# A router whose weights are stationary, with four token tiles in four column groups, and a gate summed on VectorE

## The chip, the cores and the metric

The kernel runs on one core of a Trainium2 chip. The metric is device time in microseconds: the median of the runs. The profile is of one execution. Engines in it: PE is TensorE's matmuls, PEld its weight loads, DVE is VectorE, ACT is ScalarE, POOL is GpSimd, SP is SyncE, whose queue issues most DMAs.

## The reference

4096 tokens (16 sequences of 256) of 256 channels pass a feed-forward layer, an attention layer and the same feed-forward layer again. Cut to what matters here:

```
x = x + 0.5 * ffn(layernorm(x))
x = x + attention(layernorm(x))       # 16 heads, 8 for keys and values, of 32; causal, tanh cap
x = x + 0.5 * ffn(layernorm(x))

def ffn(inp):
    h = w_norm * inp * rsqrt(mean(inp * inp) + 1e-6)
    probs = softmax(h @ w_router)                     # 256 x 32: 32 experts
    weight, chosen = top_k(probs, 4)
    out = sum over the chosen experts e, first 128 tokens of each:
          weight * (silu(h @ w_gate[e]) * (h @ w_up[e])) @ w_down[e]      # width 176
    sh = (silu(h @ sw_gate) * (h @ sw_up)) @ sw_down                      # shared expert, width 704
    return inp + out + sigmoid(h @ w_shared_gate) * sh                    # w_shared_gate: 256 x 1
```

All numbers are fp32. The change concerns `h @ w_router` and `h @ w_shared_gate`.

## The kernel before

The activations `x` stay in SBUF as 32 tiles of 128 tokens. Eight groups (`g`) of four tiles (`GT`) are the unit of routing. `route(n, g)` does one group of feed-forward layer `n` in pieces (it is a generator; a caller that advances it decides what lies between the pieces):

- moments of the four tiles on VectorE (L220, L221), their roots on GpSimd (L227, L228);
- `xr`, the rows without their mean and scaled, on VectorE (L248);
- eight transposes on TensorE into `pt` (L257), which ScalarE copies to `xnT`, times `w_norm` (L260); ScalarE also brings `x` to its normalised form (L268);
- the logits `pl` (L276): for each tile and each half of the channels one matmul, with the tile's 128x128 block of `xnT` as the stationary side and 33 columns of `wr` moving: 32 of the router and one of the shared gate;
- VectorE copies `pl` to `lg` (L280), takes the gate's column out of it (L281), then the maximum `mx` (L283) and `ex = lg - mx` (L285); ScalarE takes the exponential (L287);
- VectorE makes probabilities `pr` (L290 to L297), GpSimd puts them behind `xr` and a DMA writes both to the table `xtab` in HBM, from which experts gather rows; VectorE finds the top four and the `mask` (L303 to L307).

`slots` turns masks into lists of rows (its first matmul is `pc`, from `mask`); `expert` does one expert. `shared(g)` is the shared expert for a group: six steps of four matmuls `pg` (L390) with their activation `act` (tanh on ScalarE L394; L395 and L396 on VectorE), then four steps `po` (L402) whose sum goes to `x` (L406), scaled by `sg`, a tanh of the gate (L376). These steps serve as filling work on TensorE: `Fill.take(us)` issues steps until so many microseconds are used, and `ROUTE_FILL` and its like say how many between two pieces of another stage.

Order: TensorE follows the program's order throughout. In the first feed-forward layer a scheduler orders VectorE and ScalarE; in the attention stage all of TensorE, VectorE, ScalarE and GpSimd follow the program's order. The routing of layer 0 is the span's first 116 us, groups one after another with filling work between. The routing of layer 1 is done inside the attention loop, one piece at a time between scores (`sc`, L552), values (`den` and `y`, L598), projections (`project`: `pv` L531 with copies `v` L535, `pq` L503) and the output projection (`poa`, L616, L620). Five of its groups stand directly ahead of `pv`; groups 5 and 6 come at about 744 and 778 us, group 7 after the loop at 798 us.

PSUM: the pool `ps1` gives two buffers to everything with the tag `mm`: `pt`, `pl`, `po`, `pv`, `pq`, `poa`, `pta`, `pte`, `pc`. Whoever takes the third waits until the first is read.

## Time and profile before

| | us |
|---|---|
| median of 3 runs | 1070.91 (1069.13 to 1072.49) |
| the profiled execution | 1070.05 |
| its span | 1068.3, at a mean granted TensorE clock of 0.995 |
| TensorE busy | 1031.8 |
| VectorE busy | 628.8 |
| GpSimd busy | 499.3 |
| ScalarE busy | 399.9 |

TensorE's busy time by stage: first routing, 55.90 of the first 62 us and 53.47 of the 54 up to 116 us; experts of layer 0, 342.85 of 354 us (116 to 470); attention, 249.20 of 250 us (470 to 720) and 71.97 of 80 (720 to 800), the routing's tail among them; experts of layer 1, 228.74 of 234 us (800 to 1034); the last 34.3 us, 29.68.

A row of a group of instructions reads: line, engine, operation, output<-inputs with partitions x elements and type, how many | busy us of all, mean ns of one | idle time before them, and what ended it. The chain lists start, duration and work in the order of time; the timeline start, duration, engine, line and operation. An fp32 matmul has two records.

### The profile page before, as it was taken

What the parts mean: (1) busy time and instruction counts of PE and PEld (TensorE: products, weight loads), DVE (VectorE), ACT (ScalarE), POOL (GpSimd) and SP (SyncE); (2) the same over time, 40 slices, a digit from 0 to 9 for tenths busy, and PEclk for the clock granted to TensorE, in tenths of its full rate; (3) what the DMA queues carried; (4) which work ended last, traced back from release to release, by engine and by line L of the source; (5) the groups of instructions that cost most, each with busy time, mean ns of one, the idle gap of its engine ahead of it and who ended that gap; (6) DMA issues with size and microseconds to landing.
All of it is one profiled execution on the core that took longest, in us unless ns stands there. A gap on an engine that the chain in (4) does not pass through costs nothing.

```text
span 1068.3 us, 15597 instructions
## 1 busy us (share of the span) xinstructions
PE 1031.8 (97%) x5432; PEld 650.7 (61%) x5432; DVE 628.8 (59%) x1681; ACT 399.9 (37%) x761; POOL 499.3 (47%) x552
## 2 busy tenths in 40 slices
PE   9999999999999899999999999998999999999998
PEld 5657656777767544545455556554466567767675
DVE  5755664445343457777778777774556744443434
ACT  3343111222221246675658475756621112221210
POOL 4500102555542298788476767562311024545536
PEclk9999999999999999999999999999999999999999
DMA  9811701778773000000101010000030027777739
GB/s 297 243 69 45 233 12 48 170 159 172 168 164 58 30 21 1 20 21 2 42 1 42 2 43 1 23 1 23 25 82 23 6 56 157 163 153 170 167 55 314
DMA packets 137869, 92.97 MB, mean 87 GB/s; under 512 B 80512, under 2 KB 135104, under 8 KB 137792
## 3 DMA queue, kind: packets, MB, share of 16 engines
q1 hardware_dynamic: 125504, 74.16, 24.9%
q0 software_dynamic: 12288, 17.83, 9.7%
q8 instruction: 43, 0.70, 0.3%
q14 instruction: 34, 0.28, 0.1%
HBM read 60.99 MB, written 30.97 MB: 86 GB/s over the span
## 4 chain that ended last, share of the span: by engine, by line
PE 89%; DVE 6%; ACT 3%; issue 1%; DMA 0%; SPq 0%; POOL 0%; ACTq 0%; POOLq 0%
PE pg L390 28%; PE po L402 14%; PE pge L437 8%; PE pq L503 8%; PE poa L616 5%; PE poe L450 5%; PE sc L552 5%; PE y L598 3%; PE den L598 3%; PE pv L531 3%; PE pl L276 2%; PE pte L429 1%; PE pt L257 1%; DVE act L395 1%; DVE act L396 1%
## 5 line engine op out<-in xcount | busy, mean ns | idle before, releaser
L390 PE MATMUL pg<-xnT,sw 128*128 128x512 f32 x704 | 320.7, 600 | 1.8 <-ACT p L559 1.8
L390 PEld LDWEIGHTS pg<-xnT,sw 128*128 128x128 f32 x704 | 131.1, 192 | 138.8 <-issue 130.7
L453 POOL DMA_INDIRECT acc<-y,idx x64 | 101.4, 1584 | 183.6 <-DVE y L452 104.8
L402 PE MATMUL po<-swd,act 128*128 128x256 f32 x768 | 179.9, 383 | 6.6 <-DVE act L396 2.4
L402 PEld LDWEIGHTS po<-swd,act 128*128 128x128 f32 x768 | 143.0, 190 | 35.7 <-issue 13.0
L395 DVE SCALAR_TENSOR_TENSOR act<-act,pg 128x512 f32<-128x512 f32 x96 | 65.7, 684 | 167.9 <-ACT act L394 167.8
L394 ACT ACTIVATE act<-pg 128x512 f32<-128x512 f32 x96 | 57.2, 596 | 271.3 <-PE pg L390 271.3
L559 ACT ACTIVATE p<-sc 128x512 f32<-128x512 f32 (+1 forms) x128 | 97.4, 808 | 106.8 <-PE sc L552 106.3
L564 POOL TENSOR_SCALAR_AFFINE_SELECT p<-p 128x512 f32<-128x512 f32 x128 | 82.3, 667 | 48.1 <-ACT p L562 45.7
L413 POOL DMA_INDIRECT xg<-xtab,idx x64 | 67.9, 1061 | 76.8 <-DVE idx L368 57.9
L437 PE MATMUL pge<-xgT,wgu 128*112 128x128 f32 (+1 forms) x768 | 95.8, 275 | 5.9 <-issue 4.4
L562 ACT ACTIVATE p<-p 128x512 f32<-128x512 f32 (+1 forms) x128 | 100.9, 844 | 0.0
L437 PEld LDWEIGHTS pge<-xgT,wgu 128*112 128x112 f32 (+1 forms) x768 | 88.8, 182 | 8.7 <-issue 7.6
L552 PE MATMUL sc<-qT,kT 32*128 32x256 f32 (+1 forms) x512 | 68.5, 535 | 4.7 <-DVE act L396 3.4
L406 DVE SCALAR_TENSOR_TENSOR x<-po,sg,x 128x256 f32<-128x256 f32 x64 | 30.8, 483 | 69.2 <-PE po L402 68.9
L396 DVE TENSOR_TENSOR act<-act,pg 128x512 f32<-128x512 f32 x96 | 65.7, 685 | 2.4
L511 POOL TENSOR_TENSOR qs<-qs,kc 128x512 f32<-128x512 f32 x48 | 61.2, 1275 | 12.7 <-DVE qs L506 12.7
L432 ACT ACTIVATE xgT<-pte,wnorm 128x128 f32<-128x128 f32 x128 | 39.8, 364 | 71.3 <-PE pte L429 71.3
L450 PE MATMUL poe<-wd,sie 112*128 112x256 f32 x256 | 66.0, 380 | 0.1
L616 PE MATMUL poa<-wo,yT 128*128 128x256 f32 x256 | 59.8, 386 | 2.1 <-DVE qT L510 1.2
L503 PE MATMUL pq<-hT,wq 128*128 128x512 f32 x128 | 60.9, 600 | 0.0
L616 PEld LDWEIGHTS poa<-wo,yT 128*128 128x128 f32 x256 | 47.3, 190 | 19.8 <-ACT xnT L260 5.0
(110 smaller groups left out, 1343.7 us busy)
## 6 DMA issues: line engine op xcount, KB each, us to landing
xtab<-xr SPq DMA_DIRECT2D x16, 576.0 KB
acc<-zero SPq DMA_DIRECT2D x2, 4224.0 KB
a<-acc SPq DMA_DIRECT2D x16, 512.0 KB
wgu<-in_L_ffn_w_gate SPq DMA_DIRECT2D x64, 112.0 KB
wgu<-in_L_ffn_w_up SPq DMA_DIRECT2D x64, 112.0 KB
wd<-in_L_ffn_w_down SPq DMA_DIRECT2D x64, 112.0 KB
wgu<-in_L_ffn_w_gate SPq DMA_DIRECT2D x64, 64.0 KB
wgu<-in_L_ffn_w_up SPq DMA_DIRECT2D x64, 64.0 KB
```

What stands on the lines that cost most here:

```text
L390: nc.tensor.matmul(pg[:, s, :], lhsT=sw[:, c, w0 : w0 + P], rhs=xnT[:, c, cols], start=(c == 0), stop=(c == 1))
L395: nc.vector.scalar_tensor_tensor(si, si, 1.0, pg[:fw, 0, :], ALU.add, ALU.mult)
L402: nc.tensor.matmul(po, lhsT=act[:, k, t * P : (t + 1) * P], rhs=swd[:, k, :], start=(k == 0), stop=(k == len(FC) - 1),)
L437: nc.tensor.matmul(pg[:fw, n_, :], lhsT=wgu[:, c, w0 : w0 + fw], rhs=xgT[:, c, :], start=(c == 0), stop=(c == 1))
L450: nc.tensor.matmul(po, lhsT=si[:, k, :], rhs=wd[:, k, :], start=(k == 0), stop=(k == 1))
L453: nc.gpsimd.indirect_dma_start(out=acc[n], out_offset=bass.IndirectOffsetOnAxis(ap=idx[:, e : e + 1], axis=0), in_=y, in_offset=None, boun ...
L503: nc.tensor.matmul(pq, lhsT=weights[:, c, :], rhs=hT[:, c, :], start=(c == 0), stop=(c == 1))
L552: nc.tensor.matmul(sc[i // 2][:, i % 2, 0 : 2 * w].rearrange("p (s t) -> p s t", s=2), lhsT=kT[r, m, t0 + k0 : t0 + k0 + P], rhs=qT[r, m, ...
L559: nc.scalar.activation(parts[h], sc[h][:, :, 0 : 2 * w], AF.Tanh, scale=QK_SCALE / SOFTCAP)
L562: nc.scalar.activation(parts[h], parts[h], AF.Exp, scale=SOFTCAP)
L564: nc.gpsimd.affine_select(out=diag, in_=diag, compare_op=ALU.is_ge, fill=0.0, base=0, pattern=[[0, 4], [1, P]], channel_multiplier=-1,)
L616: nc.tensor.matmul(po, lhsT=yT[:, c // 2, c % 2, qh * P : (qh + 1) * P], rhs=wo[:, c // 2, c % 2, :], start=(c == 0), stop=(c == 3),)
```

## The change

The logits are computed the other way round: the router's weights (128x32 for each half of the channels) are stationary, and a tile's 128 tokens move. The four tiles of a group go to four column groups of the array, partitions 32t to 32t+31 of `plt`. ScalarE copies `plt` to `lt`, one transpose on TensorE makes `pl` with tokens on the partitions, and VectorE reads `mx` and `ex` from PSUM. The gate's logit is a sum over channels on VectorE: `xr` times `wg` (the gate's weights times `w_norm`, on every partition), with the accumulator written to `gate`. `wg` takes two DMAs and a multiply; `w_norm` is parked in the last tile of `x`. There is one more `yield` in `route`, and filling work is dealt out anew around it. Constants: `triu` is made from a comparison, and `last` is one column.

```diff
-ROUTE_FILL, SLOT_FILL, ... = 3.0, 1.7, ...
+ROUTE_FILL, SLOT_FILL, ... = 2.0, 1.7, ...
+LOGIT_FILL = 2.5
...
-    wr = cpool.tile([P, 2, E + 1], F32, name="wr")
-    nc.sync.dma_start(wr[:, :, 0:E], w_router.rearrange("(c p) e -> p c e", p=P))
-    nc.sync.dma_start(wr[:, :, E : E + 1], w_shared_gate.rearrange("(c p) e -> p c e", p=P))
+    wr = cpool.tile([P, 1, 2, E], F32, name="wr")
+    nc.sync.dma_start(wr[:, 0], w_router.rearrange("(c p) e -> p c e", p=P))
...
+    wg = cpool.tile([P, C], F32, name="wg")
+    nc.sync.dma_start(wg, w_shared_gate.rearrange("c e -> e c").to_broadcast([P, C]))
+    nc.sync.dma_start(x[:, NT - 1, :], w_norm.unsqueeze(0).to_broadcast([P, C]))
+    nc.vector.tensor_mul(wg, wg, x[:, NT - 1, :])
     load_x(1)
...
-    nc.vector.tensor_copy(triu, const("triu"))
+    nc.vector.tensor_single_scalar(triu, const("iota"), slot, ALU.is_ge)
...
-        pl = ps1.tile([P, GT, E + 1], F32, tag="mm", name="pl")
+        plt = ps1.tile([P, 1, P], F32, tag="mm", name="plt")
+        for s in range(1):
+            for c in range(2):
+                for t in range(GT):
+                    i = g * GT + t
+                    nc.tensor.matmul(
+                        plt[E * t : E * (t + 1), s, :], lhsT=wr[:, s, c, :], rhs=xnT[:, c, i * P : (i + 1) * P],
+                        start=(c == 0), stop=(c == 1),
+                    )
+        lt = stat.tile([P, 1, P], F32, name="lt", bufs=1)
+        nc.scalar.copy(lt, plt)
         for t in range(GT):
             i = g * GT + t
-            for c in range(2):
-                nc.tensor.matmul(
-                    pl[:, t, :], lhsT=xnT[:, c, i * P : (i + 1) * P], rhs=wr[:, c, :], start=(c == 0), stop=(c == 1)
-                )
-        lg = stat.tile([P, GT, E + 1], F32, name="lg", bufs=2)
-        nc.vector.tensor_copy(lg, pl)
-        nc.vector.tensor_copy(gate[:, g * GT : (g + 1) * GT], lg[:, :, E])
+            junk = stat.tile([P, C], BF16, name="junk", bufs=1)
+            nc.vector.scalar_tensor_tensor(
+                junk, xr[:, t, 0:C], 1.0, wg, ALU.mult, ALU.mult, accum_out=gate[:, i : i + 1]
+            )
+        yield 0.8
+        pl = ps1.tile([P, 1, GT, E], F32, tag="mm", name="pl")
+        for s in range(1):
+            nc.tensor.transpose(pl[:, s].rearrange("p t e -> p (t e)"), lt[:, s, :], ident)
         mx = stat.tile([P, GT, 1], F32, name="mx")
-        nc.vector.tensor_reduce(mx[:, :, 0], lg[:, :, 0:E], AX.X, ALU.max)
+        nc.vector.tensor_reduce(mx[:, :, 0], pl[:, 0], AX.X, ALU.max)
         ex = stat.tile([P, GT, E], F32, name="ex", bufs=2)
-        nc.vector.tensor_sub(ex, lg[:, :, 0:E], mx.to_broadcast([P, GT, E]))
-        yield 1.9
+        nc.vector.tensor_sub(ex, pl[:, 0], mx.to_broadcast([P, GT, E]))
+        yield 0.2
...
-        nc.tensor.matmul(pn, lhsT=const("last"), rhs=hib.rearrange("p h i -> p (h i)"), start=True, stop=True)
+        nc.tensor.matmul(
+            pn, lhsT=const("last").to_broadcast([P, P]), rhs=hib.rearrange("p h i -> p (h i)"), start=True, stop=True
+        )
...
     def shared(pool, g, last):
-        sg = stat.tile([P, GT], F32, name="sg")
-        nc.scalar.activation(sg, gate[:, g * GT : (g + 1) * GT], AF.Tanh, scale=0.5)
-        nc.vector.tensor_scalar(sg, sg, 1.0, 0.125, ALU.add, ALU.mult)
...
         for k, (f0, fw) in enumerate(FC):
+            if k == 3:
+                sg = stat.tile([P, GT], F32, name="sg")
+                nc.scalar.activation(sg, gate[:, g * GT : (g + 1) * GT], AF.Tanh, scale=0.5)
+                nc.vector.tensor_scalar(sg, sg, 1.0, 0.125, ALU.add, ALU.mult)
...
             fill.take(ROUTE_FILL)
+            next(work)
+            fill.ready = g + 1
+            fill.take(LOGIT_FILL)
             advance(work, 2)
             advance(later[2])
-            fill.ready = g + 1
             fill.take(ROUTE_FILL)
             next(work)
...
+            if j == 1:
+                advance(routing.get(g - 2))
+                if mine is None:
+                    spare_time(LOGIT_FILL)
```

More of the change, by code (lines that the diff above doesn't have):

```diff
@@ L40 @@
 ET = mybir.EngineType
-ROUTE_FILL, SLOT_FILL, FIRST_FILL, EXPERT_FILL, SUM_FILL, PROJECT_FILL = 3.0, 1.7, 6.0, 2.4, 17.0, 1.5
+ROUTE_FILL, SLOT_FILL, FIRST_FILL, EXPERT_FILL, SUM_FILL, PROJECT_FILL = 2.0, 1.7, 6.0, 2.4, 17.0, 1.5
 LAST_FILL = 8.0
@@ L54 @@
 _n = 0
-for _name, _w in [("ident", P), ("cos", T), ("sin", T), ("triu", P), ("iota", CAP),
-                  ("ustrict", P), ("last", P), ("block", P // NT), ("slot", 1), ("spare", 1), ("base", 1)]:
+for _name, _w in [("ident", P), ("cos", T), ("sin", T), ("iota", CAP),
+                  ("ustrict", P), ("last", 1), ("block", P // NT), ("slot", 1), ("spare", 1), ("base", 1)]:
     _COLS[_name] = (_n, _w)
@@ L76, in _constants @@
     put("sin", np.tile(np.sin(emb).T * sign[:, None], (P // HD, 1)))
-    put("triu", np.triu(np.ones((P, P))))
     put("iota", np.tile(np.arange(CAP) + 0.5, (P, 1)))
@@ L83, in _constants @@
     put("ustrict", blocks * np.triu(np.ones((P, P)), 1))
-    put("last", np.tile(p % NT == NT - 1, (1, P)))
+    put("last", p % NT == NT - 1)
     put("block", p // NT == np.arange(P // NT))
```

## The prediction

> **What bounds the kernel now.** I read first the busy times and the chain that ended last, on the page.
>
> ```profile
> PE 1031.8 (97%) x5432; PEld 650.7 (61%) x5432; DVE 628.8 (59%) x1681; ACT 399.9 (37%) x761; POOL 499.3 (47%) x552
> ...
> PE 89%; DVE 6%; ACT 3%; issue 1%; DMA 0%; SPq 0%; POOL 0%; ACTq 0%; POOLq 0%
> ```
>
> TensorE is busy 1031.8 of 1068.3 us; less TensorE work is the only large lever, and it pays only where TensorE then does not wait. Second, the groups of instructions, for what the change takes out and for its nearest relatives.
>
> ```profile
> L276 PE MATMUL pl<-wr,xnT 128*128 128x33 f32 x256 | 30.9, 275 | 0.9 <-ACT xnT L260 0.7
> L620 DVE TENSOR_TENSOR x<-poa,x 128x256 f32<-128x256 f32 x32 | 12.7, 416 | 14.0 <-PE poa L616 13.9
> L306 DVE MATCH_VALUE_LOAD hit<-top,pr 128x8 f32 x64 | 5.3, 83 | 0.4
> L295 DVE TENSOR_TENSOR ex<-ex,tot 128x128 f32<-128x128 f32 x16 | 4.6, 290 | 0.3
> L297 DVE SCALAR_TENSOR_TENSOR pr<-ex 128x128 f32<-128x128 f32 x16 | 4.6, 289 | 0.4
> ```
>
> Third, the chain from 586 to 606 us, the place in the attention stage where one of five router groups stands in front of the values' projection.
>
> ```profile
> 589.37 1.29 PE y L598 x16
> 590.66 0.43 PE den L598 x8
> 591.09 3.65 PE pv L531 x16
> 594.74 1.71 PE pl L276 x16
> 596.45 1.07 PE sc L552 x8
> 597.52 3.63 PE pq L503 x8
> ```
>
> One group's logits take 1.71 us: 16 passes (an fp32 matmul is recorded as two) at 107 ns. TensorE works there without a gap. Fourth, VectorE's timeline at the same place, columns start and duration:
>
> ```profile
> 592.94 0.69 DVE L606 TENSOR_TENSOR yT<-y,rb 128x512 f32<-128x512 f32 x1
> 593.55 0.68 DVE L535 COPY v<-pv 128x512 f32<-128x512 f32 x1
> 594.78 0.69 DVE L535 COPY v<-pv 128x512 f32<-128x512 f32 x1 [0.55 <-PE pv L531]
> ...
> 597.52 0.26 DVE L280 COPY lg<-pl 128x132 f32<-128x132 f32 x1
> ...
> 598.21 0.29 DVE L285 TENSOR_TENSOR ex<-lg,mx 128x128 f32<-128x128 f32 x1
> ```
>
> VectorE has no gap here except 0.55 us: it is the second busy engine of this stretch, in a fixed order. Fifth, the chain near 40 us, in the first routing:
>
> ```profile
> 41.23 0.58 DVE act L395
> ...
> 42.12 0.69 DVE act L396
> ...
> 43.06 0.69 PE po L402 x2
> ```
>
> There TensorE waits for VectorE; between 26 and 38 us VectorE is busy 12.00 of 12.00 us.
>
> **TensorE's part.** Removed: 16 groups x 1.71 = 27.4 us. Added: 16 passes of 128 moving columns in four column groups. No row has that shape. The den row beside it has the same array form (128*32): 8 passes of 256 columns in 0.43 us, four at a time; half the columns and twice the passes gives 0.43 us again. Lower bound 0.34 (pc's 16 bf16 passes took that), upper 1.71 if the groups don't overlap; I take 0.43. The transpose back costs 0.11 (pt: four in 0.44). A change of array form costs 0.14 (den after sc, 0.57 against 0.43) to 0.24 (pv after den, 3.65 against 3.41), so two make 0.40. The Trainium skill, page "TensorEngine Tiling (Array Packing)", section "Overview", puts four column tiles at up to 4x; taken of the 1.71 us this too is 0.43, without the switches and the transpose that the rows add. So a group gains 1.71-0.54-0.40 = 0.77 us, and 1.17 for six that follow den, where that switch was paid already: 10 x 0.77 + 6 x 1.17 = 14.7 us, if nothing waits.
>
> **VectorE's part.** Removed for each group: the copies lg (0.28) and gate (0.17). Added: four accumulating SCALAR_TENSOR_TENSOR of 256 columns, all writing one junk tile, so each waits for the one before. Call the four S. The plain operation at this width is near 0.42 us (L620, 416 ns), at best 0.34 from start to start where neighbours overlap by 0.08: S is at least 1.4. The skill's page "VectorE: DVE Perf Modes", section "Two Vector instructions with no wait between them", says an operation that writes out its accumulator is two instructions; the nearest small companion in the trace is MATCH_VALUE_LOAD, 83 ns. That gives 0.50 each, S = 2.0, my value. A rule against the change: "Vector Engine (DVE) Microarchitecture Reference", section "Points that are easy to get wrong", says this operation with two non-bf16 SBUF sources runs at half throughput. The row to weigh is L297: both sources fp32 in SBUF, 289 ns, the same as a plain TENSOR_TENSOR (L295, 290). It shows no halving, but it has no accumulator. By the rule the 256 columns take some 0.27 us more (from the rows' slope, (416-290) ns per 128 columns, doubled), 0.70 each, S = 2.8: the upper end.
>
> **The five groups in front of pv.** In the new order VectorE runs yT, the four accumulations, two v copies, the moments of four tiles, mx, ex. The transpose's pl and the first pq take both buffers that the second pq needs, so that one waits for ex. From yT's end as pipelined, 593.55: S, two copies 1.22, moments 2.14, mx and ex 0.62: ex ends at 597.53+S. TensorE reaches the second pq at 599.27 in the timeline of before, and would do so at 598.1 with 1.17 saved. The net gain is thus 599.24-597.53-S = 1.71-S. With S = 2.0 each of the five is 0.29 slower: +1.5 us in all, in place of -5.9. With S = 1.4 it is -1.6, with S = 2.8 it is +5.5. Also there, a po that follows waits for act on VectorE, which at 606.66-608.07 was just in time: +0.7, once.
>
> **First routing, 0 to 62 us.** TensorE gains 0.77 in each of three groups before 43 us, but the first po waits for act, and VectorE gets more work ahead of it: twelve accumulations (6.0), the multiply for wg (0.4, L620's row), and the second group of x some 0.9 us later, because two more DMAs (128 KB each; SP's queue spends 0.47 us on each issue) go ahead of it. Leaving its way are lg and gate of three groups (1.3) and, by the new order, xr, lg, gate and mx of the fourth (2.0). The excess, 4.0, meets VectorE's idle time between 14 and 43 us (1.8 before 20, 0.35 before 26, 0.9 at 39: 3.1). So po comes 0.9 later, near 44 us, and TensorE's 2.3 become waiting. Behind it one group gains 0.8 and pays 0.6 for lt, ScalarE's copy, which stands between plt and the buffer of the next po; without lg and gate the mask is ready 0.5 earlier, on which the pt at 60.93 depends. Together +0.2. The constants' transfer gets 130 KB shorter, off the path; the gate's own DMA (0.47 on the queue) goes, already counted against the new ones.
>
> **62 to 116 us.** Four groups, -3.1. In the last one the filling work is split in two by pl: between pl and the mask's matmul pc lie 3.44 us of pg instead of 6.95, and mx to mask with an act between takes 5.2 (54.94 to 59.22 less lg and gate is 3.8, plus 1.4 of act): +1.8. Waits for lt +0.3. Together -1.0.
>
> **The last three groups** (744 to 800 us): group 5 keeps 0.8; group 6 keeps 1.1: in the new order a pg step covers the stall near 786 us (po waits for x, 1.53), and a new wait of po for ex takes part of that back; group 7, whose pl directly follows plt, waits 0.6 for lt: -0.2.
>
> The tanh of the gate moved to the fourth step of the shared expert, and triu by comparison instead of a copy, cost nothing: ScalarE is at 37%, and TensorE's pg steps (3.44 us) cover them.
>
> **Sum:** +0.2 - 1.0 + 1.5 + 0.7 - 0.8 - 1.1 - 0.2 = -0.7 us. Against the profiled execution, 1070.05, that is 1069.35; the median of the runs lies 0.86 above that execution, so 1070.2.
>
> **Rivals.**
> - *The saving arrives.* For: TensorE is the bound by every view, and 470 to 720 us has 249.20 of 250 us busy. Against: VectorE's chain in front of the second pq. With S = 1.4 the five groups give -1.6 and the first po comes 1.1 earlier than assumed: the sum is -4.9, 1066.0. If the second pq did not wait for ex at all, and the first po came earlier by what TensorE saved, up to -14.7: 1056.
> - *VectorE pays double (other side).* Place: four accumulations in front of the v copies. Price: S = 2.8, +5.5 instead of +1.5, and 12 x 0.2 = 2.4 us more ahead of the first po: sum +5.7, 1076.6. It decides (over 0.3%) from S about 2.5 on.
> - *Column groups don't overlap.* plt takes 1.71: +1.28 a group. In the five groups that hides behind VectorE; in eight others it is exposed: +10 less what waits swallow, about +7, 1077. The den row speaks against it.
> - *A wait that I don't see,* such as the reused pair of small PSUM buffers holding po: 1074 to 1080.
>
> **How the numbers follow.** 0.3% (3.2 us) is about what a measurement of this kernel can tell from no change: 1067.7 to 1074.1. Chances: no net change 0.38, S small 0.20, whole saving 0.08, VectorE double 0.22, no overlap 0.05, unseen wait 0.07. Faster: the whole saving, most of S small and a tenth of the likeliest, 0.29; slower: the last three and a little of the likeliest, 0.35; same 0.36. The likeliest's own range is 1066 to 1074; the range for 8 in 10 is 1059 to 1079.
>
> **What would show it.** Right: plt's 16 passes in about 0.43 us; the accumulations at 0.45 to 0.5 us; TensorE's busy time down by some 15 us, with its idle time up by nearly as much; idle before pq with ex as what ended it, five times 1 us or more; idle before pc near 112 us; the first po at 43 to 44 us. Wrong: accumulations at 0.7 us; plt over 0.8; no idle before pq, so that the time is below 1062; or the second pq not the place where TensorE waits.

## The result, and the profile after

The changed kernel takes 1075.51 us in the median (1070.71 to 1077.59, 7 runs); the kernel before, run beside it, 1070.91 (1067.0 to 1072.71, 7 runs). The ratio is 1.005, with a 95% interval of 1.0034 to 1.0065: about 5 us slower, where I had forecast no change at 1070.2. The profiled execution of the changed kernel took 1077.19 us, its span 1075.5 at a mean granted clock of 0.991.

The page, with the busy times and then the shares of the chain that ended last:

```profile
PE 1022.4 (95%) x5448; PEld 629.4 (59%) x5448; DVE 647.6 (60%) x1778; ACT 404.7 (38%) x777; POOL 498.2 (46%) x549
...
PE 78%; DVE 13%; ACT 3%; DMA 2%; issue 2%; POOL 1%; SPq 1%; POOLq 0%; ACTq 0%; DVEq 0%
```

TensorE works 9.4 us less, and the span is 7.2 us longer: 16.6 us of new idle time (from here on, figures of the two traces; the medians differ by less). VectorE holds 13% of the chain in place of 6%. The groups of instructions that the change added:

```profile
L292 DVE SCALAR_TENSOR_TENSOR junk<-xr,wg 128x256 bf16<-128x256 f32 x64 | 26.9, 420 | 1.3
L283 PE MATMUL plt<-xnT,wr 128*32 128x128 f32 x256 | 11.3, 277 | 1.8 <-ACT xnT L265 1.8
L292 DVE DVE_READ_ACCUMULATOR junk<-xr,wg 128x1 f32 x64 | 5.2, 82 | 0.0
L298 PE MATMUL pl<-kc,lt 128*128 128x128 f32 x16 | 4.8, 301 | 5.5 <-DVE v L555 4.3 <-ACT lt L288 1.2
```

An accumulation is two instructions, 420 and 82 ns: 0.50 us, the value taken. The column groups do overlap: 11.3 us for 16 groups, 0.71 each as modelled, against 1.71 before. The idle time ahead of `pl` ends on `v`, VectorE's copy ahead of it, 4.3 us in all.

The same work in the two traces shows where the time went. The first attention's `yT` starts at 408.14 us, before at 405.14: +3.0. After the five router groups in front of `pv` it is +4.25 (724.48 against 720.23). The last mask starts at 811.07 against 805.74, +5.3; the last expert's `y` starts at 1039.37 against 1033.20, +6.2; the last addition to `x` at 1071.61 against 1064.30, +7.3. So of the 5.3 us lost by the masks 3.0 are lost before the attention stage, 1.2 over the stretch with the five groups, and the rest behind them.

The five groups first, TensorE's timeline at one of them (the idle time ahead and what ended it stand in brackets):

```profile
594.27 0.62 PE L283 MATMUL plt<-xnT,wr 128*32 128x128 f32 x16
594.82 3.72 PE L551 MATMUL pv<-wv,hT 128*128 128x256 f32 x16
599.40 0.33 PE L298 MATMUL pl<-kc,lt 128*128 128x128 f32 x1 [0.86 <-DVE v L555]
599.66 1.14 PE L572 MATMUL sc<-qT,kT 32*128 32x512 f32 x8
600.73 1.98 PE L523 MATMUL pq<-hT,wk 128*128 128x512 f32 x4
602.72 1.96 PE L523 MATMUL pq<-hT,wq 128*128 128x512 f32 x4
```

TensorE is done with `pv` at 598.54 and waits 0.86 us for a buffer that VectorE's copy of `v` has to free. VectorE's timeline at the same place:

```profile
596.91 0.41 DVE L292 SCALAR_TENSOR_TENSOR junk<-xr,wg 128x256 bf16<-128x256 f32 x1
597.25 0.08 DVE L292 DVE_READ_ACCUMULATOR junk<-xr,wg 128x1 f32 x1
...
598.66 1.28 DVE L555 COPY v<-pv 128x512 f32<-128x512 f32 x2
...
602.29 0.29 DVE L302 TENSOR_TENSOR ex<-pl,mx 128x128 f32<-128x128 f32 x1
```

Four accumulations hold it from 596.91 to 598.66, ahead of the two copies. `ex` ends at 602.58, just before the second `pq` starts at 602.72. The saving turns into a wait on VectorE, as forecast; only the place is one step earlier.

Now the start. VectorE's first instructions of the changed kernel, and then of the kernel before:

```profile
14.22 0.43 DVE L148 TENSOR_TENSOR wg<-wg,x 128x256 f32<-128x256 f32 x1 [5.58 <-DMA x<-in_L_ffn_w_norm]
15.97 0.75 DVE L225 BATCH_NORM_STATS2 st<-x 128x6 f32<-128x256 f32 x2
```

```profile
12.56 0.75 DVE L220 BATCH_NORM_STATS2 st<-x 128x6 f32<-128x256 f32 x2 [3.82 <-DMA x<-in_L_attn_X]
```

VectorE stands 5.58 us until the broadcast of `w_norm` has landed, and the moments of the second group start at 15.97, not 12.56. I had taken 0.9 us for this. The DMA view shows why; 40 slices of 0.2 us from 6 to 14 us, after and before:

```profile
GB/s 397 410 410 410 332 319 402 389 371 384 397 397 371 318 227 218 164 129 109 70 113 72 54 90 77 82 61 51 97 118 87 128 154 169 189 174 210 256 312 318
```

```profile
GB/s 358 410 410 397 397 402 278 345 430 371 358 397 358 371 346 319 246 277 329 335 356 358 353 379 394 369 379 394 379 374 364 358 353 338 343 292 225 287 266 276
```

From 9.6 to 12.4 us the transfers move 51 to 128 GB/s, where they moved some 350 before. That is the time of the two loads that repeat a 1 KB row on 128 partitions. They count as 128 KB each, but hold the transfers back for nearly 3 us, in which a megabyte moved before. (Two of the expectations below quote 14.12 and 16.05 us and 76 to 136 GB/s for this place; the trace shown here has 14.22, 15.97 and 51 to 128.) From there on VectorE is behind, and TensorE waits for it:

```profile
20.25 0.67 PE L262 MATMUL pt<-kc,xr 128*128 128x128 f32 x4
25.64 0.64 PE L262 MATMUL pt<-kc,xr 128*128 128x128 f32 x4 [4.71 <-DVE ex L302]
```

What that costs by the end of the first routing is read at the first transpose of the fifth group. Ahead of it TensorE has done the same filling work in both kernels (52 records of `pg` and 48 of `po`). After, and before:

```profile
63.35 1.87 PE L262 MATMUL pt<-kc,xr 128*128 128x128 f32 x8 [2.58 <-DVE xr L253]
```

```profile
60.93 1.12 PE L257 MATMUL pt<-kc,xr 128*128 128x128 f32 x4 [2.52 <-DVE xr L248]
```

That is 2.4 us.

And a gap costs more than its length. Windows of the changed kernel (from:to, length, busy time of PE, PEld, DVE, ACT and POOL with counts, granted clock, DMA share, GB/s):

```profile
20.50:25.50 5.00, 0.42 (x4) 0.18 (x2) 3.51 (x14) 2.55 (x5) 1.31 (x4) 1.00 1.10 352
26.00:30.00 4.00, 4.00 (x8) 1.73 (x7) 4.00 (x22) 1.99 (x6) 2.84 (x6) 0.57 0.37 131
722.00:729.00 7.00, 5.93 (x30) 2.48 (x24) 3.99 (x8) 3.01 (x6) 1.23 (x2) 1.00 0.00 0
729.00:733.00 4.00, 4.00 (x24) 1.00 (x26) 3.44 (x19) 2.54 (x3) 0.79 (x2) 0.57 0.42 147
755.00:762.00 7.00, 5.05 (x14) 2.03 (x16) 5.05 (x13) 4.17 (x8) 5.37 (x11) 1.00 0.00 0
763.00:767.00 4.00, 4.00 (x12) 3.17 (x12) 0.43 (x1) 2.80 (x3) 1.27 (x2) 0.57 0.00 0
```

TensorE stands for 4.58 us of the first window at full clock; the four microseconds that follow are granted 0.57, which loses up to 1.7 us more. The same at 729 and 763, after windows with one or two microseconds of idle time. The Trainium skill, page "TensorE: Matmul & The Clock Gate", Part 1, section "What's actually happening", describes a gate with half rate after an idle window of about 3.4 us. 4 us at 0.57 are 3.44 us at one half and the rest at full clock, so rate and length agree; the idle window does not, since before 729 and 763 no gap is longer than 1.10 us.

Those two stretches are not the change's own, though. The kernel before has the same gaps; its trace has no stretch after them. But another trace of that kernel has both, in a run whose program differs only behind the attention stage ("Less filling work", below). TensorE's timeline and a window of the kernel before:

```profile
724.53 1.13 PE L552 MATMUL sc<-qT,kT 32*128 32x512 f32 x4 [1.07 <-DVE act L396]
```

```profile
726.50:733.00 6.50, 4.80 (x38) 1.96 (x31) 4.26 (x11) 5.27 (x10) 2.98 (x4) 1.00 0.26 93
```

The same of that other run:

```profile
722.21 1.13 PE L552 MATMUL sc<-qT,kT 32*128 32x512 f32 x4 [1.07 <-DVE act L396]
```

```profile
728.00:732.00 4.00, 3.82 (x5) 1.70 (x6) 1.30 (x2) 3.61 (x8) 1.22 (x2) 0.57 0.02 4
```

So one and the same gap brings a stretch in one execution and none in another. In the traces' clock records the stretches of one execution lie on a grid of 3.41 us (26.12, 63.66, 729.26 and 763.39 us here are 11, 195 and 10 such steps apart), and the grid lies elsewhere in each execution. That this decides which gaps are hit is my reading and not tested. Ahead of its tail the changed kernel's trace has these four stretches, and the trace of the kernel before has three (13, 61 and 399 us). What the clock takes must therefore be read from many executions.

### The profile page after: what moved, and what is told of

It reads as the page before. It is cut to its first block, busy times and chain, and to the rows that moved or that the text cites. A ratio compares the mean times of both kernels' runs of the same rounds, so it can differ in the third digit from the quotient of the medians.

```text
span 1075.5 us, 15765 instructions
## 1 busy us (share of the span) xinstructions
PE 1022.4 (95%) x5448; PEld 629.4 (59%) x5448; DVE 647.6 (60%) x1778; ACT 404.7 (38%) x777; POOL 498.2 (46%) x549
## 4 chain that ended last, share of the span: by engine, by line
PE 78%; DVE 13%; ACT 3%; DMA 2%; issue 2%; POOL 1%; SPq 1%; POOLq 0%; ACTq 0%; DVEq 0%
PE pg L410 24%; PE po L422 13%; PE pge L457 8%; PE pq L523 7%; PE poa L636 5%; PE poe L470 5%; PE sc L572 5%; PE y L618 3%; PE den L618 3%; DVE act L415 2%; DVE junk L292 1%; DVE act L416 1%; DMA a<-acc 1%; DVE st L225 1%; PE pte L449 1%
```

## The experiments

The theories behind the expectations are these. *Start*: the two broadcast loads make the first group of VectorE's work late. *VectorE*: the four accumulations stand ahead of `v` and `ex`, and TensorE waits for a small PSUM buffer. *Clock*: the gaps on TensorE bring half-clock stretches. *End*: the lost time is given back or taken in the last expert's filling work. Each ratio is to the kernel before on the same chip, with its interval. The mean granted clock of the timed runs is given where it bears on the reading; time lost by clock is estimated as (1 - clock) times the mean time. That is an upper estimate, because half-clock time in which TensorE has nothing to do, as at the end of the span, counts in it; over the 149 executions of the kernel before on record, which ran beside the experiments, 0.001 of clock goes with 0.92 us, where the estimate has 1.07. By it the kernel before (0.9950, 1070.4 us in these executions) loses 5.3 us to the clock and the changed one (0.9926, 1075.3, 7 executions) 8.0: of its 5 us, some 2.7 may be clock. Seven executions leave that open from 0.4 to 4.9.

### The start

**The two loads alone, added to the kernel before** (nothing reads them before the tiles of `x` are overwritten):

```diff
+    nc.sync.dma_start(x[:, NT - 2, :], w_shared_gate.rearrange("c e -> e c").to_broadcast([P, C]))
+    nc.sync.dma_start(x[:, NT - 1, :], w_norm.unsqueeze(0).to_broadcast([P, C]))
     load_x(1)
```

> The kernel before with one thing added: the two DMAs that spread a row of 1 KB over 128 partitions (the gate's weights and w_norm), at the changed kernel's place ahead of the second group of x, into tiles of x that are loaded later; nothing reads them. Theory D (these two DMAs are slow for their 128 KB each: in the changed kernel's trace the rate falls to 76 to 136 GB/s while they run, and x's second group is there only about 16.0 us): the first moments of the second group start near 15.9 instead of 12.56 us, TensorE idles 1 to 3 us more before 30 us, and the time rises by 1.5 to 4 us, to about 1071 to 1074. The prediction's own figure (x 0.9 us later, hidden): no change.

1072.82 us, ratio 1.0029 (1.0013 to 1.0044): +3.1 us, at an unchanged clock (0.9948). VectorE's and TensorE's timelines in this kernel:

```profile
15.92 0.75 DVE L222 BATCH_NORM_STATS2 st<-x 128x6 f32<-128x256 f32 x2 [7.31 <-DMA x<-in_L_attn_X]
```

```profile
20.06 0.67 PE L259 MATMUL pt<-kc,xr 128*128 128x128 f32 x4 [2.95 <-DVE xr L250]
```

The moments start within 0.05 us of where the changed kernel has them, and TensorE waits 2.95 us for `xr`. So the loads alone cost 3 us, without any of the change's arithmetic. At the fifth group's first transpose this kernel is 2.5 us late (63.44).

**The loads earlier**, ahead of the shared expert's weights:

```diff
     nc.sync.dma_start(wr[:, 0], w_router.rearrange("(c p) e -> p c e", p=P))
+    wg = cpool.tile([P, C], F32, name="wg")
+    nc.sync.dma_start(wg, w_shared_gate.rearrange("c e -> e c").to_broadcast([P, C]))
+    nc.sync.dma_start(x[:, NT - 1, :], w_norm.unsqueeze(0).to_broadcast([P, C]))
```

> The changed kernel with the two DMAs that make wg issued right after the router's weights, ahead of the shared expert's. Theory A (the start: VectorE stands until 14.12 us at the multiply for wg, because w_norm lands 8.1 us after its issue, so the moments of the second group begin at 16.05 instead of 12.56 us): the multiply then starts before 9 us, those moments near 13, TensorE's 4.7 us of idle time before 25.6 us shrink to under 2, and the time falls by 2 to 3 us, to about 1073. Rival B (it is the accumulations' own 32 us on VectorE): under 1 us. Rival C (it is where the filling work lies and the clock in the tail): no change.

1076.97 us, 1.0068 (1.0043 to 1.0092): no gain. The multiply for `wg` came at 10.72, but the first `pt` at 11.53, not 7.7, and the moments of the second group at 16.09. The low rate moves with the loads: in this trace it is 36 to 115 GB/s from 6.0 to 8.2 us. Wherever the loads stand, what is queued behind them is late.

**One row in place of 128.** Two loads of 1 KB to one partition, the product there, a matmul with a row of ones that spreads it to 128 partitions, and a copy (the warming matmuls are moved ahead of it):

```diff
-    nc.sync.dma_start(wg, w_shared_gate.rearrange("c e -> e c").to_broadcast([P, C]))
-    nc.sync.dma_start(x[:, NT - 1, :], w_norm.unsqueeze(0).to_broadcast([P, C]))
-    nc.vector.tensor_mul(wg, wg, x[:, NT - 1, :])
+    nc.sync.dma_start(row[:, 0], w_shared_gate.rearrange("c e -> e c"))
+    nc.sync.dma_start(row[:, 1], w_norm.unsqueeze(0))
+    nc.gpsimd.memset(lead, 1.0)
+    nc.vector.tensor_mul(row[:, 0], row[:, 0], row[:, 1])
...
+    nc.tensor.matmul(pb, lhsT=x[0:1, NT - 3, 0:P], rhs=row[:, 0], start=True, stop=True)
+    nc.scalar.copy(wg, pb)
```

> The changed kernel with wg made otherwise: two DMAs of 1 KB to one partition, one multiply there, one matmul with a row of ones that spreads it over the partitions, and a copy by ScalarE. Theory D: the second group of x is there by 13.5 us, VectorE no longer stands at the multiply, the 4.7 us of idle TensorE before 25.6 us shrink below 1.5, and the time falls by 3 us or more, to 1070 to 1073. Theory C (filling work and tail): no change.

1075.45 us, 1.005 (1.0033 to 1.0066): no gain either, although the slow loads are gone (from 6 to 14 us the rate stays at 230 GB/s or more). VectorE's and TensorE's timelines:

```profile
11.81 0.75 DVE L231 BATCH_NORM_STATS2 st<-x 128x6 f32<-128x256 f32 x2 [0.61 <-DMA x<-in_L_attn_X]
...
41.65 1.38 DVE L259 TENSOR_SCALAR xr<-x,mv,s 128x256 f32<-128x256 f32 x4 [1.21 <-DMA xtab<-xr]
```

```profile
31.48 0.67 PE L268 MATMUL pt<-kc,xr 128*128 128x128 f32 x4 [2.24 <-DVE xr L259]
...
43.60 4.39 PE L428 MATMUL po<-swd,act 128*128 128x256 f32 x12 [2.15 <-DVE x L432]
```

The second group's moments start at 11.81, earlier than before the change, and TensorE waits a little later instead, for `xr`, and then for `x`. VectorE in turn waits for the table's write to release `xr`. By the last mask the kernel is 1.2 us ahead of the changed one (110.86 against 112.11 in the first layer), and has lost that again by the first attention's `yT` (408.76 against 408.14); half-clock stretches at 44, 61, 160 and 403 us lie on the way, where the changed kernel's trace has two, at 26 and 64. The late load was one cause; a second one lay behind it. It is not simply VectorE's added work: the waits for `xr` and `x` are there without the accumulations too (TensorE's part alone, below).

### VectorE's accumulations

**Without them.** The gate's logit is left out (zero), all else is as changed:

```diff
-        for t in range(GT):
...
-            nc.vector.scalar_tensor_tensor(
-                junk, xr[:, t, 0:C], 1.0, wg, ALU.mult, ALU.mult, accum_out=gate[:, i : i + 1]
-            )
```

> The changed kernel without the 64 accumulating instructions; the gate is set to zero once, so the part left out is the shared gate's logit (wg is still loaded and multiplied). Theory B (their time on VectorE takes the saving back): five groups gain 1.0 to 1.5 us each and the first routing 2 to 4 us, in all 7 to 10, about 1067. Theory A (most of it is lost at the start by the wait for w_norm): 4 to 6 us, about 1070, with the multiply for wg still ending near 14.5 us and a stall of TensorE near 22 us that stays over 2 us.

1075.69 us, 1.0047 (1.0026 to 1.0068). Leaving 32 us of VectorE's work out gains nothing in the end. In the five groups the wait ahead of `pl` is gone, and the second `pq` waits instead:

```profile
606.51 1.96 PE L518 MATMUL pq<-hT,wq 128*128 128x512 f32 x4 [0.42 <-DVE ex L297]
```

So there the forecast's wait, `pq` for `ex`, is real, at 0.42 us (with S at nothing). But the start did not get better: the loads are still there (the multiply at 13.75), the scheduler ordered VectorE anew, and the last `act` of layer 0's filling work starts at 369.70, against 363.86 in the changed kernel and 360.84 before. Its clock is 0.9890: by the estimate 11.8 us are lost by it. The run does not measure the accumulations' price, because the first routing changed with them (the fifth group's first transpose comes at 66.44).

**Without them and without their loads**: TensorE's part alone, the gate's logit left out again. On top of the last edit:

```diff
-    nc.sync.dma_start(wg, w_shared_gate.rearrange("c e -> e c").to_broadcast([P, C]))
-    nc.sync.dma_start(x[:, NT - 1, :], w_norm.unsqueeze(0).to_broadcast([P, C]))
-    nc.vector.tensor_mul(wg, wg, x[:, NT - 1, :])
```

> TensorE's part alone: no accumulations and no loads for them (the gate's logit is left out, zero), all else as changed. Without the accumulations but with the loads it was 1075.7 us. If the loads are the cause of the late start there, this is 3 us less or better, 1072 or below, and the first pt has no wait above 1 us before 30 us. If VectorE's order, made anew by the scheduler, or the shorter clock-gated stretches hold the time, the start is early again but the time stays at 1074 or more at a clock of 0.990 or less. If the saving of TensorE's part arrives when nothing else is added, 1060 to 1066.

1070.8 us, 0.9997 (0.9979 to 1.0014). The loads are thus worth some 5 us where VectorE has no sums. And TensorE's part, with nothing else added and VectorE relieved of two copies a group, is no faster than the kernel before: the expected 1060 to 1066 fail. TensorE's timeline of this kernel at the start, and a window:

```profile
30.63 0.67 PE L259 MATMUL pt<-kc,xr 128*128 128x128 f32 x4 [1.53 <-DVE xr L250]
...
43.38 5.49 PE L413 MATMUL po<-swd,act 128*128 128x256 f32 x12 [2.73 <-DVE x L417]
```

```profile
42.00:50.00 8.00, 6.62 (x20) 5.19 (x20) 5.04 (x27) 2.63 (x6) 5.64 (x13) 0.57 1.02 337
```

What TensorE saves in the first groups it waits for VectorE's `xr` and `x`, and the eight microseconds from 42 are granted 0.57, up to 3.4 us lost. The fifth group's first transpose comes at 62.98, 2.05 us later than before: the first routing loses time even without the loads and the sums. At its clock of 0.9902 this kernel loses 10.5 us, against 6.0 of the kernel before on the same chip; the rest, 1061.2 against 1065.2 us, holds all that the smaller TensorE work brings: by this estimate 4 us of the forecast 14.7, and the clock takes them. The run has the new division of the filling work as well; no run separates that from the matmuls.

**After `ex`**, the four accumulations moved behind the subtraction:

> The changed kernel with the four accumulations of a group issued after ex instead of before the transpose. In the attention stage they then lie behind mx and ex in VectorE's order. If the prediction's sum for the five groups is right (ex ends at 597.53 + S), each of the five gains up to 1.2 us less what the next piece of VectorE loses (the late sums plate, the act before po): 2 to 5 us in all, about 1071 to 1073. If VectorE's amount of work and not its order is what counts there: 0 to 1 us. The first routing, whose order a scheduler makes, should change little.

```diff
         nc.vector.tensor_sub(ex, pl[:, 0], mx.to_broadcast([P, GT, E]))
+        for t in range(GT):
...
+            nc.vector.scalar_tensor_tensor(
+                junk, xr[:, t, 0:C], 1.0, wg, ALU.mult, ALU.mult, accum_out=gate[:, i : i + 1]
+            )
```

1077.39 us, 1.0068 (1.0045 to 1.0091). TensorE's timeline:

```profile
602.02 1.96 PE L523 MATMUL pq<-hT,wq 128*128 128x512 f32 x4 [0.41 <-DVE ex L296]
...
606.93 0.64 PE L618 MATMUL den<-plate,ones 128*32 128x256 f32 x8 [0.45 <-DVE plate L594]
```

The wait only moves, from `pl` to `pq` and on to `den`: behind `ex` the accumulations are no better placed than ahead of `v`.

**A buffer of its own for `pl`**, from the pool's other pair:

```diff
-        pl = ps1.tile([P, 1, GT, E], F32, tag="mm", name="pl")
+        pl = ps1.tile([P, 1, GT, E], F32, tag="aux", name="pl")
```

> The changed kernel with the transpose's result pl in the pair of small PSUM buffers with the tag aux, so that pl neither waits for a buffer of pv nor holds one until ex. Theory A2 (the held buffer turns VectorE's lateness into TensorE's waiting): the idle time of TensorE before pt at 25.6 us gets shorter, the 0.86 us before pl and the wait of the second pq in the five groups of the attention stage go, and each of the five gains 0.3 to 1 us; together 3 to 5 us, about 1071. Rival B (VectorE itself is the limit there, and the next thing that it is late for takes over the wait): under 1.5 us.

1078.19 us, 1.007 (1.0045 to 1.0094). The waits ahead of `pl` and `pq` are gone in the five groups, and there this kernel gains 4.0 us (`yT` at 494.38 and then at 723.00, in the changed kernel at 491.89 and 724.48), although a `po` waits 1.53 us for `act`. The gain is lost at both ends. It comes 2.5 us late into the stretch, and behind it `y` waits 3.32 us for `ex` (up to 754.78), for which VectorE does four accumulations and the moments first. The half-clock stretches at 25 and 62 us are twice as long as the changed kernel's, and the clock is 0.9860: by the estimate 15.1 us are lost by it, and 1062.5 us are left, against 1067.3 of the changed kernel. In its trace a quarter of the half-clock time lies at the very end, where TensorE is idle, so that this is not shown.

**The accumulations beside the transposes**, on top of the row in one partition: they run in the piece of `route` with the first four transposes, ahead of the logits.

```diff
+            if h == 0:
+                for t in range(GT):
...
+                    nc.vector.scalar_tensor_tensor(
+                        junk, xr[:, t, 0:C], 1.0, wg, ALU.mult, ALU.mult, accum_out=gate[:, i : i + 1]
+                    )
```

> The same as the run with the row, and the four accumulations of a group moved ahead, to the piece with the first two tiles' transposes, where VectorE in the attention stage stands idle for 2 us. Expected, if S in front of the v copies costs what the prediction said: the wait of pl for v (0.86 us) goes and a wait of the second pq for ex of 0.4 us is left, as in the run without accumulations; five groups gain 0.5 to 1 us each, 2 to 4 us below the run with the row. If VectorE's amount of work counts: nothing.

1071.71 us, 1.0014 (1.0002 to 1.0025): 3.7 us less than the row alone. The same move in the changed kernel itself, with the broadcast loads kept:

> The changed kernel with the accumulations beside the first four transposes of a group, and the two broadcast loads kept. Beside the row in one partition this move was worth 3.7 us. If the two causes simply add, it is worth the same here: 1071.8 us, ratio 1.0015. If the accumulations' place matters only once the late load is gone, because VectorE stands for the load first, it is worth less than 1.5 us: 1074 or more, ratio above 1.0035. If the accumulations now stand behind the multiply for wg and make the first group's wait longer, it is slower than the changed kernel, 1077 or more.

1073.97 us, 1.0025 (1.0012 to 1.0038): some 2.7 us less than the changed kernel, between the two expectations. The accumulations now start at 14.25, behind the multiply, and the second group's moments at 15.77, as late as before the move; the gain comes later. In the five groups the wait ahead of `pl` is gone and one of `pq`, 0.42 us, is left; over that stretch it is 2.8 us better than the changed kernel (721.81 against 724.48, from a start 0.2 us later), and its last mask starts at 807.78 instead of 811.07. So the accumulations' place costs by itself. The row gains nothing at the old place; at the new one its ratio is lower by 1.1 in a thousand, but the intervals overlap, so that its gain is not shown in the time.

**Both, with `pl` in the other pair**, and then **in the other pair only for layer 0 and the first five groups**, since in the first of these `y` waited 1.57 us for `ex` behind them (up to 747.85):

```diff
-        pl = ps1.tile([P, 1, GT, E], F32, tag="aux", name="pl")
+        pl = ps1.tile([P, 1, GT, E], F32, tag="aux" if n == 0 or g < 5 else "mm", name="pl")
```

> The same as the run with the row and the moved accumulations, and pl in the buffers with the tag aux. Expected: no wait in front of pl and none of the second pq for ex; 1 to 3 us below the run before it, about 1064 to 1068, faster than the kernel before. If TensorE's waits only move on (to the late sums' den or to po's act): the same as the run before it.

> The kernel with the row, the moved accumulations and pl with the tag aux, but aux only where it does not collide with den and y: the first routing and groups 0 to 4 of the second; groups 5 to 7 have mm as in the changed kernel. In the run before, y waited 1.57 us for ex at 747.9 and den 0.39 for yT. Expected: these waits go and 1 to 2 us with them, about 1069; a rival says that the granted clock takes it back: the same 1071.

1071.18 us, 1.0001 (0.9989 to 1.0013), and 1069.49 us, 0.9985 (0.9972 to 0.9998). With these three places mended the change is no loss any more. The steps in one table. Where the intervals of two rows overlap, as those of neighbouring rows mostly do, the rows are not shown to differ:

| kernel | ratio to before | mean clock |
|---|---|---|
| the two loads alone, in the kernel before | 1.0029 | 0.9948 |
| TensorE's part alone | 0.9997 | 0.9902 |
| and the loads | 1.0047 | 0.9890 |
| and the accumulations: the change | 1.0050 | 0.9926 |
| the change, accumulations beside the transposes | 1.0025 | 0.9915 |
| the change, one row | 1.0050 | 0.9927 |
| the change, both | 1.0014 | 0.9915 |
| both, `pl` in the other pair | 1.0001 | 0.9915 |
| the same, up to group 4 in layer 1 | 0.9985 | 0.9915 |

### TensorE's part and the clock

**TensorE's part undone**: 32 columns of weights move, with tokens stationary, at the transpose's place; loads and accumulations stay.

```diff
-                        plt[E * t : E * (t + 1), s, :], lhsT=wr[:, s, c, :], rhs=xnT[:, c, i * P : (i + 1) * P],
...
-            nc.tensor.transpose(pl[:, s].rearrange("p t e -> p (t e)"), lt[:, s, :], ident)
+                    pl[:, 0, t, :], lhsT=xnT[:, c, i * P : (i + 1) * P], rhs=wr[:, 0, c, :], start=(c == 0), stop=(c == 1)
```

> The changed kernel with TensorE's part undone: logits as in the kernel before (tokens stationary, 32 columns moving, at the transpose's place), no plt, no lt, no transpose; the accumulations, the DMAs for wg and the order of the filling work stay. It shows what TensorE's part is worth in this kernel. If it is worth its 14.7 us: 1088 or more. If it is worth what is left after the waits in the five groups (about 0 there) and in the first routing: 1077 to 1081. If TensorE's saving is all swallowed: 1074 to 1077.

1098.82 us, 1.0262 (1.0242 to 1.0281). So in this kernel TensorE's part is worth 23 us, more than the 14.7 of its sum, and everything else together costs 28. TensorE's timeline at the same router group, and a window:

```profile
609.59 1.97 PE L289 MATMUL pl<-wr,xnT 128*128 128x32 f32 x16 [1.30 <-DVE v L548]
```

```profile
612.00:616.00 4.00, 4.00 (x12) 1.40 (x5) 3.80 (x13) 3.06 (x4) 3.33 (x5) 0.57 0.00 0
```

Here `pl` waits 1.30 us for `v`, up to 609.59, and from 612 on the clock is at 0.57. This follows in four of the five groups (502.5, 612, 666.5 and 718 us). The changed kernel's 0.86 us gaps at the same place were followed by none. The clock is 0.9828: by the estimate 18.9 us are lost by it, 11 more than in the changed kernel, which is half of the 23.

**Gaps filled.** Eight small matmuls on zeros, whose result nobody reads, in the gaps between 726 and 762 us of the changed kernel:

```diff
+                if i == 2 and w == T and u[0] == NG - 1:
+                    spin((2, 1, 0, 2)[2 * b + m])
...
+            if w < T and u[0] == NG - 1:
+                spin((1, 0, 2, 0)[2 * b + m])
```

> The changed kernel with eight small matmuls of zeros added, into a tile that nothing reads, at five places between 726 and 762 us where TensorE stands still for 0.6 to 1.1 us (before the second half of sc and before pg). They do no work; they only fill gaps. Theory E (the granted clock: TensorE's new idle time makes it fall to half for 3.4 us at a time, 1.71 us lost each; the changed kernel's profile has such stretches at 729 and 763 us, the kernel before has none there): these two go, the mean granted clock rises by about 0.003, and the time falls by 1.5 to 3.4 us, to 1072 to 1074, although TensorE has more to do. Rival (the waits alone count, the clock is an accident of the profiled run): no change, or 0.5 us slower.

1076.46 us, 1.0049 (1.003 to 1.0068). Windows of this kernel:

```profile
722.00:729.00 7.00, 7.00 (x38) 3.07 (x28) 3.78 (x7) 3.23 (x6) 1.23 (x2) 1.00 0.00 0
729.00:733.00 4.00, 3.04 (x33) 1.01 (x34) 3.66 (x20) 2.82 (x4) 1.05 (x2) 1.00 0.40 142
763.00:767.00 4.00, 4.00 (x28) 2.99 (x30) 0.85 (x2) 2.57 (x4) 1.27 (x2) 1.00 0.00 0
```

Both stretches are at full clock. The last mask starts 1.9 us earlier (809.15), the last `y` starts 1.3 earlier (1038.03), and the last addition to `x` starts at 1071.56, as in the changed kernel (1071.61). In this trace the gain was made and given back at the end of the span. The median did not move, and the mean clock, 0.9926, is that of the changed kernel: the expected rise of 0.003 did not come. So over many executions this run does not show that these gaps cost time; the expectation's rival, that the clock of the profiled execution was an accident, is not excluded by it.

### The end of the span

The last pieces of the changed kernel's timeline show what holds the end (1028 to 1080 us):

```profile
1063.77 2.29 DVE L767 TENSOR_TENSOR x<-x,a 128x256 f32<-128x256 f32 x1 [5.94 <-DMA a<-acc]
1066.50 4.54 PE L422 MATMUL po<-swd,act 128*128 128x256 f32 x12 [4.02 <-DVE x L426]
```

VectorE, in order, stands 5.94 us until the experts' sums `a` are read back from HBM, and TensorE's last `po` waits behind it for 4.02. Before, TensorE's filling work ran through to 1063.75. From the last `y` to the end of the span it is 36.1 us, and 35.1 before.

**Less filling work between the last experts**, more behind them: 2.2 us for each expert in layer 1, not 2.4. The same edit was made to the changed kernel, to the kernel before and to the best version (below), there with 2.0 too.

```diff
-                fill.take(EXPERT_FILL)
+                fill.take(EXPERT_FILL if n == 0 else 2.2)
```

> The changed kernel with 2.2 instead of 2.4 us of filling work behind each expert of the second layer: 34 x 0.2 = 6.8 us of pg and po move from before the last expert to behind it. Theory F (the end is the last expert's scatter-add, the reading of the sums and what follows, some 36 us behind the last y, with TensorE idle for several us meanwhile): the last y comes 5 to 6 us earlier, the time falls by 3 to 6 us, to 1070 to 1072.5. Rival (TensorE's total counts wherever it lies): no change, within 1 us.

> The kernel before with the same move (2.2 instead of 2.4). Theory F: there the end is TensorE's own remaining filling work, without idle time from 1034 to 1063 us; the last y comes 5 to 6 us earlier, TensorE ends at the same time, and the time stays within 1.5 us of 1069.5. If the end hung on the last expert there too: 3 to 6 us faster.

> The best version so far (row, moved accumulations, pl in aux where it fits, zeros in the gaps: 1067.85) with 2.2. Its last y lies at 1028.7 us and TensorE idles some 10 us behind it. Theory F: 3 to 6 us faster, 1062 to 1065. Rival: the same 1068.

> The same with 2.0: 13.6 us moved, more than TensorE's idle time behind the last expert. Theory F: the bound turns back to TensorE's total; no better than with 2.2, 1061 to 1066.

Changed kernel: 1076.15 us, 1.0059 (1.0041 to 1.0077). Before: 1084.73, 1.014 (1.0117 to 1.0164). Best version: 1070.08, 0.9997 (0.9983 to 1.0012), and with 2.0 it is 1085.26, 1.015 (1.0126 to 1.0174). TensorE's timeline of the kernel before with this edit, at its end:

```profile
1058.90 10.72 PE L390 MATMUL pg<-xnT,sw 128*128 128x512 f32 x20 [10.56 <-DVE act L396]
```

The work that was moved does not run in the shadow of the reading: its `act` stands on VectorE behind the additions that wait for it. In the kernel before TensorE waits 10.56 us, in the changed one 4.98. The last `y` comes only 2.4 us earlier there (1030.83), not the expected 5 to 6. None of the splits tried gains.

### A version faster than both

The best of the above with the filled gaps: the row in one partition, the accumulations beside the transposes, `pl` in the other pair up to group 4 of layer 1, and the eight matmuls on zeros.

> The run before it with the eight small matmuls of zeros in the gaps between 720 and 762 us. Theory E: the two stretches of half clock there go, mean granted clock up by about 0.003, 1.5 to 3.4 us faster, about 1066 to 1068, faster than the kernel before. Rival: no change.

1067.85 us, 0.9976 (0.9966 to 0.9986): 2.6 us faster than the kernel before. Against the same version without the zeros (1069.49 on the same chip) that is 1.6 us. The zeros are no part of the change, and the kernel before, which has these gaps too, was not given them; what they are worth there is open. The five groups in this version, TensorE's timeline:

```profile
592.42 0.27 PE L305 MATMUL pl<-kc,lt 128*128 128x128 f32 x1
...
595.51 1.88 PE L530 MATMUL pq<-hT,wq 128*128 128x512 f32 x4
...
605.48 0.67 PE L429 MATMUL po<-swd,act 128*128 128x256 f32 x2 [1.08 <-DVE act L423]
```

Neither `pl` nor `pq` waits; one `po` still waits 1.08 us for VectorE. Its clock is 0.9921: by the estimate 8.4 us are lost by it, 3 more than before the change. At equal clock it is some 5 us faster (1059.8 against 1065.5 us on the same chip), and half of that goes to the clock.

## Why the prediction was wrong

The terms of the sum beside the two traces. A term is measured as the growth of the lag of the changed kernel, in us:

| stretch | forecast | measured |
|---|---|---|
| first routing, to the fifth group's first transpose | +0.2 | +2.4 |
| from there to `pc` (112.42 against 114.18, with one step of 3.44 us of filling work still to do) | -1.0 | -0.7 |
| from `pc` to the first attention's `yT` | 0 | +1.3 |
| the five groups | +1.5 + 0.7 | +1.2 |
| the last three groups, to the last mask | -2.1 | +1.1 |
| experts of layer 1, to the last `y` | 0 | +0.9 |
| from there to the last addition to `x` | 0 | +1.1 |

*TensorE's part, -14.7.* The mechanism held: the column groups overlap. 16 passes took 0.55 us up to the next start, with the switches at their ends, where the prediction's two ways to 0.43 us (the den row, and an estimate from the up to 4x that the Trainium skill, page "TensorEngine Tiling (Array Packing)", section "Overview", gives) left these out. The transpose was 0.27 to 0.33 with its switch. Busy time fell by 9.4. TensorE's busy time under half clock grew from 10.2 to 17.1 us; half of that taken off leaves a fall of 12.8, as an estimate. The rival "column groups don't overlap" falls.

*VectorE's part, S = 2.0.* 420 + 82 ns each, four in 1.75 us from start to start: right within 0.25, and the rival "VectorE pays double" falls with its rule of half throughput: the accumulating operation with two fp32 sources takes 420 ns, the plain one of the same width 416. That this rival's time, 1076.6, lies near the measured one is chance.

*The five groups, +0.29 each.* Measured +0.16, +0.17, +0.54 (there with the forecast `po` behind `act`, 0.44 us), +0.17 and +0.17. The forecast named the wait of `pq` for `ex`; it is the wait of `pl` for `v`, 0.86 us, that comes first, and `ex` is the next in line (0.42 in the run without sums). Near in size, wrong by one step in place. Sum 1.2, forecast 1.5 + 0.7.

*62 to 116 us.* The stall of `pc` for the mask was 1.61 us at 112.42, forecast 1.8: right.

*First routing, +0.2: failed.* The sum said "the second group of x some 0.9 us later, because two more DMAs (128 KB each ...)". It was 3.4 us, since those loads ran at 51 to 128 GB/s; I had priced a load by its bytes and by its time on the issuing queue. The path was wrong too: not the first `po` waits for `act` (it starts at 42.36 without a wait), but `pt` for `ex`, 4.71 us up to 25.64. The whole term measured +2.4. The loads alone make the kernel before 2.5 us late at the same mark, and cost it 3.1 us in the end; with that in the place of +0.2 the sum is about +2.2. They are not the only cause: without loads and sums the mark is still 2.05 us late.

*The clock: left out, without a reason.* The whole sum was made at an unchanged clock. A gap can be followed by 3.41 us at half clock that cost up to 1.7 us more. The mean clock of the timed runs fell by 0.0025, which the estimate makes 2.7 us. Which gaps bring this about is not shown: of the four stretches ahead of the tail two follow gaps that the kernel before has too. "An unseen wait (1074 to 1080)" is the rival that came true in its time only.

*The last three groups and the tail.* The sum has -2.1 for groups 5 to 7; measured, the lag between the five groups and the last mask grew by 1.1 (+4.25 to +5.3), with the stretches at 729 and 763 in it, up to 3.4 us. Without these it would be near the forecast. Behind it a further 2 us went, 0.9 of it by the last `y` and 1.1 in a tail whose end moved from TensorE's filling work to the additions on VectorE. The sum had nothing for either. It had nothing for the experts of layer 0 either; there TensorE waits 1.31 us for `row` ahead of `pa` (158.5 to 160.3), where before filling work lay in between.

*The rival "the saving arrives"* asked only that S be small. TensorE's part alone has S = 0 and no loads, and ends at 0.9997: even then the saving goes into waits for `xr` and `x` in the first routing, and, by the estimate, to the clock.

So the failed step that is shown is the price of the two loads in the first routing: 3.4 us in place of 0.9, by the loads alone, by their form (11.81 against 16.09 for the next moments, one row against the broadcast at the same place) and by their removal where there are no sums. The fall of the mean clock is shown as a measurement; that it comes from the change's own gaps is argued. How the first 116 us divide between the late load, VectorE's added work, its newly scheduled order and the new division of the filling work is not settled: the edits there changed the scheduler's order too, and no run has TensorE's part with the old division. The split of the 5 us into clock and waits rests on the mean clock alone.

## What to carry to other kernels

An engine at 97% can be relieved by 15 us and the kernel still lose time: ask of every microsecond saved which engine sets the next start, and count the idle time it leaves with what the clock takes afterwards. Price a load by its form, not by its bytes alone: as a load ahead of the data everybody waits for, the row repeated on 128 partitions made these 3.4 us late; as one row and a matmul with ones it did not. Where several causes lie one behind another, undoing one can show nothing (the row alone, 1.005). And before a stretch of half clock is put down to a gap, look whether the other kernel has the same gap.

## What was not expected of the hardware

- Two loads of a 1 KB row to 128 partitions kept the DMA rate at 51 to 128 GB/s for nearly 3 us, and delayed the next load by 3.4 us.
- One gap of 1.3 us on TensorE was followed by half clock in four of five places; gaps of 0.86 us at the same place, in none. A gap of 1.07 us in the same code was followed by 4 us at 0.57 in one execution and by none in another. The stretches of one execution start whole steps of 3.41 us apart.
- A little less filling work between the last experts (24 records of `po` more behind them; twelve take 2.86 us here) cost the kernel before 15 us: TensorE waited 10.56 us for an `act` that stood on VectorE behind the additions of the sums.
